# Conditioned adapter with residual layer norm: the order of the first loads and of the start-up work

## The chip, the cores and the metric

The kernel runs on one core of one Trainium2 chip. The metric is the device time of one execution in microseconds; the median of three executions is compared. A core has five engines with a queue of instructions each: PE (matrix products, into PSUM), DVE (vector work), ACT (activations and copies), POOL (elementwise work on SBUF) and SP (which here only issues transfers). ACT can issue transfers too. In the profile SP's transfers stand as queue q1 and ACT's as q10.

## What is computed

There are 128 sequences (B) of 128 positions (S) with 512 features (H), in float32. Each sequence has an id that picks one of L = 10 sets of adapter parameters. Cut to what matters:

```python
w1 = W1[language_ids]                  # (B, 512, 128)
w2 = W2[language_ids]                  # (B, 128, 512)
h = relu(einsum('bsh,bha->bsa', x, w1) + b1[language_ids][:, None, :])
adapted = einsum('bsa,bah->bsh', h, w2) + b2[language_ids][:, None, :]
r = x + adapted
mean = r.mean(-1); var = ((r - mean) ** 2).mean(-1)
normed = (r - mean) * rsqrt(var + 1e-5)
out = x + normed * gamma[language_ids][:, None, :] + beta[language_ids][:, None, :]
```

## The kernel before

**Loads.** All parameters stay in SBUF for the whole run: W1 as one tile `w1` (2.62 MB, loaded in four quarters of 640 KB by the 128-row blocks of H, in runs of 512 B, L95 to L99), W2 as one tile `w2` (two transfers of 1.3 MB, L101 to L107), the tables beta, gamma and b2 in one tile `rows` (30 rows of 2 KB, L86 to L88), b1 (`b1r`, L90) and the ids (L85). x is loaded in tiles of four sequences; the first tile, `x_0`, comes in two halves (L82, L83), the others by `load_x` (L67), with four buffers. The order on the two issuing queues is:

- SP: ids, gamma, first half of x_0, W1 quarters 0 and 1, second half of x_0, W2, x_1, x_2, x_3
- ACT: beta, b2, b1, W1 quarters 2 and 3

A helper `keep` chains the instructions of one engine, so each engine runs them in the order of the source from L85 on.

**Start-up.** DVE clamps the ids (L120 to L123) and splits the 30 table rows into three bf16 parts (L134 to L138, `parts`), and makes a selection matrix `pick` (L131, L132). Then each of the 30 rows is spread over all 128 partitions (`spread`, L152): PE multiplies a column of `pick` by `parts` into a PSUM buffer (pool `p_y`, five buffers, shared with the products of the main loop), and DVE or ACT copies it to `beta_b`, `gamma_b` or `b2_b`. `spin` (L306) issues products of no use on PE.

**Main work of one sequence b.** `transpose_x` puts x[b] into PSUM by four products with the identity (pool `p_x`, one buffer); `copy_xT` (ACT) copies it to SBUF; `stage_w1` (ACT) copies the picked set out of `w1`; `down` runs four products into `p_h` (one buffer; each float32 product shows as two instructions in the profile); `relu` (ACT) makes `hT`; `up` runs the product with `w2`, and for some sequences a product that adds b2; `residual` (DVE, L238) adds x and sums; `square` and `deviation` (ACT) and some small DVE steps give the norm; `scale` and `finish` (DVE, L282 and L291) make the output; POOL adds b2 to x (L202) and beta to x (L209) beforehand; `store` writes two sequences at a time.

**The order of the start.** It is written out by hand from L316 to L344: 12 spins, the transposes of sequence 0, b1's transpose, 22 rows spread (the transposes of sequence 1 after the sixth, then a half spin after each row), two sets of W1 staged, four spins, then down(0) to down(2) with the transposes of sequences 2 and 3 and the last eight rows, up(0), up(1), down(3). The loop from L346 on then runs each stage of the following sequences in turn, with down one sequence and up two behind the transposes.

Of the kernel before, what the change touches and what calls it, by code (L numbers as in the profile page):

```python
# [16 lines left out]
P = 128  # L17
# [6 lines left out]
def cond_resid_kernel(ctx: ExitStack, tc: tile.TileContext, x, itok, W1, b1, W2, b2, gamma, beta, out):  # L24
# [8 lines left out]
    nc = tc.nc  # L33
    B, S, H = x.shape
    L, _, A = W1.shape
    KC = H // P
# [6 lines left out]
    def keep(ins):  # L43

        engine = ins.ins.engine
        if engine in last:
            tc.add_manual_dep(ins.ins, last[engine], behind, reason="kept order")
        last[engine] = ins.ins.name
        return ins
# [20 lines left out]
    def xb(b):  # L70
        return xs[b // G][:, b % G, :]


    ids = const.tile([1, B], I32, name="ids")
    rows = rp.tile([P, H], FP, tag="r", name="rows")
    b1r = const.tile([L, A], FP, name="b1r")
    w1 = const.tile([P, L, KC, A], FP, name="w1")
# [4 lines left out]
    def load_part(lo, hi):  # L82
        keep(nc.sync.dma_start(out=x_0[:, lo:hi, :], in_=x[lo:hi].rearrange("b s h -> s b h")))  # L83

    keep(nc.sync.dma_start(out=ids, in_=itok.rearrange("(o b) -> o b", o=1)))  # L85
    keep(nc.scalar.dma_start(out=rows[0:L, :], in_=beta))  # L86
    keep(nc.sync.dma_start(out=rows[L : 2 * L, :], in_=gamma))
    keep(nc.scalar.dma_start(out=rows[2 * L : 3 * L, :], in_=b2))  # L88
    load_part(0, 2)
    keep(nc.scalar.dma_start(out=b1r, in_=b1))  # L90

    warm = const.tile([P, 1], FP, name="warm")
    nc.vector.memset(warm, 1.0)
    keep(nc.scalar.activation(warm, warm, AF.Sqrt))
    for k in range(KC):  # L95
        queue = nc.sync if k < 2 else nc.scalar
        keep(
            queue.dma_start(out=w1[:, :, k, :], in_=W1[:, k * P : (k + 1) * P, :].rearrange("l p a -> p l a"))
        )  # L99
    load_part(2, G)  # L100
    for l in range(0, L, 5):  # L101
        keep(
            nc.sync.dma_start(
                out=w2[:, l * H : (l + 5) * H].rearrange("p (l h) -> p l h", l=5),
                in_=W2[l : l + 5].rearrange("l a h -> a l h"),
# [20 lines left out]
    R = 3 * L  # L126
# [25 lines left out]
    def spread(r, copier):  # L152
        t = (beta_b, gamma_b, b2_b)[r // L]
        row = p_y.tile([P, H], FP, tag="y", name=f"row_{r}")
        pick_r = pick[:, r : r + 1].to_broadcast([96, P])
        keep(nc.tensor.matmul(row, lhsT=pick_r, rhs=parts[:96, :], start=True, stop=True))
        dst = t[:, r % L * H : (r % L + 1) * H]
        if copier is nc.scalar:
            keep(nc.scalar.copy(dst, row))
        else:  # L160
            keep(nc.vector.tensor_copy(dst, row))  # L161
# [4 lines left out]
    def lid(b, engine):  # L166
        g = b // G
        if (g, engine) not in lids:
            loads, vals = nc.values_load_multi_w_load_instructions(
                lang[0:1, g * G : (g + 1) * G],  # L170
                engines=[engine],
                min_val=0,
                max_val=L - 1,
                skip_runtime_bounds_check_because="clamped on the chip to 0..L-1 above",
            )
            for ins in loads:
                keep(ins)
            lids[g, engine] = vals
        return lids[g, engine][b % G]
# [4 lines left out]
    def stage_w1(b):  # L184
        w1s[b] = wp.tile([P, KC, A], FP, tag="w1s", name=f"w1s_{b}")
        src = w1.rearrange("p l k a -> p (l k a)")[:, bass.ds(lid(b, ET.Activation) * (KC * A), KC * A)]
        keep(nc.scalar.copy(w1s[b].rearrange("p k a -> p (k a)"), src))  # L187

    def transpose_x(b):
        pxs[b] = p_x.tile([P, KC, P], FP, tag="xT", name=f"pxT_{b}")  # L190
        for k in range(KC):
            keep(nc.tensor.transpose(pxs[b][:, k, :], xb(b)[:, k * P : (k + 1) * P], ident))  # L192

    def copy_xT(b):
        xT[b] = tp.tile([P, KC, P], FP, tag="xT", name=f"xT_{b}")
        keep(nc.scalar.copy(xT[b], pxs.pop(b)))  # L196
# [14 lines left out]
    def down(b):  # L211
        phs[b] = p_h.tile([P, P], FP, tag="h", name=f"ph_{b}")
        for k in range(KC):
            keep(
                nc.tensor.matmul(  # L215
                    phs[b], lhsT=w1s[b][:, k, :], rhs=xT[b][:, k, :], start=(k == 0), stop=(k == KC - 1)
                )
            )
        del xT[b], w1s[b]

    def relu(b):
        hT[b] = tp.tile([P, P], FP, tag="hT", name=f"hT_{b}", bufs=6)
        keep(nc.scalar.activation(hT[b], phs.pop(b), AF.Relu, bias=b1T[:, bass.ds(lid(b, ET.Activation), 1)]))  # L223

    def up(b):
        v = lid(b, ET.PE)
        ys[b] = p_y.tile([P, H], FP, tag="y", name=f"py_{b}")
        m = b2_by_matmul(b)
        if m:
            pick_b = pick[:, bass.ds(v + 2 * L, 1)].to_broadcast([96, P])  # L230
            keep(nc.tensor.matmul(ys[b], lhsT=pick_b, rhs=parts[:96, :], start=True, stop=False))  # L231
        keep(nc.tensor.matmul(ys[b], lhsT=hT[b], rhs=w2[:, bass.ds(v * H, H)], start=not m, stop=True))  # L232
        del hT[b]
# [72 lines left out]
    def spin(n, width):  # L306
        idle = p_s.tile([P, H], FP, tag="s", name="idle")
        for _ in range(n):
            keep(
                nc.tensor.matmul(  # L310
                    idle[:, :width], lhsT=ones, rhs=ones[:, 0:1].to_broadcast([P, width]), start=True, stop=True
                )
            )


    spin(12, H)  # L316
    transpose_x(0)
    transpose_b1()
    copy_xT(0)
    for r in range(22):  # L320
        spread(r, nc.scalar if r % 3 == 2 else nc.vector)
        if r == 5:
            transpose_x(1)
            copy_xT(1)
        elif r > 5:
            spin(1, H // 2)
    stage_w1(0)
    stage_w1(1)
    spin(4, H)
    for b in range(3):  # L330
        down(b)
        if b < 2:
            transpose_x(b + 2)
        relu(b)
        if b < 2:
            copy_xT(b + 2)
        for r in range(22 + 3 * b, min(25 + 3 * b, R)):
            spread(r, nc.vector)
        stage_w1(b + 2)
    up(0)  # L340
    up(1)
    down(3)
    relu(3)
    stage_w1(5)  # L344

    for i in range(3, B + U + 7):  # L346
        if i < B and i % G == 0 and i // G + 3 < NG:
            load_x(i // G + 3)
        b = i - U - 1
# [21 lines left out]
        p = g - 1  # L371
# [77 lines left out]
```

## Time and profile before

| What | Value |
| --- | --- |
| Three executions | 322.06, 322.19, 323.7 us, median 322.19 |
| The profiled execution's own time | 324.36 us |
| Its span, first to last instruction | 322.5 us |
| Mean granted PE clock | 0.984 of full |
| Busy share PE, DVE, ACT, POOL | 95%, 94%, 87%, 85% |
| Moved by DMA | 72.89 MB, mean 226 GB/s |

The profiled execution is one of its own, a little longer than the median. Some lines of the page, with the busy time of a group, the mean of one in ns, and the idle time of its engine just before with what ended it:

```profile
DVE  6928899999999999999999999999999999999994
ACT  3436999999999999999999999999999999999950
POOL 1306999999999999999999999999999999999900
...
L209 POOL TENSOR_TENSOR o<-x,beta_b 128x512 f32<-128x512 f32 x128 | 162.2, 1280 | 10.0 <-DVE beta_b L161 10.0
L202 POOL TENSOR_TENSOR r<-x,b_b 128x512 f32<-128x512 f32 x93 | 118.9, 1279 | 21.7 <-DVE b_b L161 13.4
L187 ACT COPY w1s<-w 128x512 f32 x128 | 79.3, 620 | 3.3 <-DMA w<-in_L_cond_W_dram 3.2
```

The first three lines are the busy tenths of an engine in 40 slices of some 8 us: DVE, ACT and POOL are filled from the fifth slice on, and the gaps lie in the first four. The groups say that POOL waits twice for spread rows and that ACT waits once for W1, in the start as well.

### The profile page before, as it was taken

How to read it: one execution, taken by the hardware profiler on the slowest of the kernel's cores; microseconds unless marked ns; L12 is line 12 of the kernel's file. 1: busy time of each engine (PE TensorE's matmuls, PEld its weight loads, DVE VectorE, ACT ScalarE, POOL GpSimd, SP SyncE). 2: the span in 40 equal slices, each digit the busy share in tenths (PEclk: the TensorE clock that was granted, in tenths of full speed). 3: DMA queues.
4: the chain of work that ended last, by engine and by line, in shares of the span. 5: the costliest groups of instructions: out<-in, count | busy, mean ns of one | idle time of the engine just before them, and what ended most of it. 6: DMA issues, size and time to landing. Idle time of an engine off the chain costs nothing. (4 is left out here: it accounts for less than half of the span.)

```text
span 322.5 us, 7159 instructions
## 1 busy us (share of the span) xinstructions
PE 305.1 (95%) x1889; PEld 227.0 (70%) x1890; DVE 303.8 (94%) x996; ACT 280.6 (87%) x713; POOL 274.7 (85%) x229
## 2 busy tenths in 40 slices
PE   8869999999999999999999999999999999999950
PEld 3456777777777777777777777777777777777720
DVE  6928899999999999999999999999999999999994
ACT  3436999999999999999999999999999999999950
POOL 1306999999999999999999999999999999999900
PEclk9979999999999999999999999999999999999995
DMA  7997467776666666777576666777766666633333
GB/s 207 323 384 268 186 210 259 262 259 226 210 217 223 242 229 227 261 262 251 192 231 221 235 242 224 238 262 261 244 216 212 229 227 239 221 117 131 130 125 139
DMA packets 40955, 72.89 MB, mean 226 GB/s; under 512 B 1705, under 2 KB 6836, under 8 KB 40914
## 3 DMA queue, kind: packets, MB, share of 16 engines
q1 hardware_dynamic: 38262, 71.07, 64.2%
q10 hardware_dynamic: 2652, 1.36, 1.7%
q8 instruction: 16, 0.26, 0.4%
q14 instruction: 25, 0.20, 0.2%
HBM read 38.86 MB, written 33.55 MB: 225 GB/s over the span
## 5 line engine op out<-in xcount | busy, mean ns | idle before, releaser
L209 POOL TENSOR_TENSOR o<-x,beta_b 128x512 f32<-128x512 f32 x128 | 162.2, 1280 | 10.0 <-DVE beta_b L161 10.0
L215 PE MATMUL ph<-xT,w1s 128*128 128x128 f32 x1024 | 136.3, 276 | 3.0 <-ACT w1s L187 3.0
L202 POOL TENSOR_TENSOR r<-x,b_b 128x512 f32<-128x512 f32 x93 | 118.9, 1279 | 21.7 <-DVE b_b L161 13.4
L232 PE MATMUL py<-w,hT 128*128 x256 | 131.1, 593 | 0.8 <-ACT sq L250 0.8
L215 PEld LDWEIGHTS ph<-xT,w1s 128*128 128x128 f32 x1024 | 125.5, 193 | 4.7 <-ACT w1s L187 3.5
L192 PEld LDWEIGHTS pxT<-ident,x 128*128 128x128 f32 x512 | 64.1, 141 | 66.7 <-issue 43.7
L282 DVE SCALAR_TENSOR_TENSOR py<-py,nmean,gamma_b 128x512 f32<-128x512 f32 x128 | 96.2, 752 | 0.3 <-issue 0.3
L291 DVE SCALAR_TENSOR_TENSOR o<-py,rstd,o 128x512 f32<-128x512 f32 x128 | 94.7, 741 | 1.1
L250 ACT ACTIVATE sq<-py,nmean 128x512 f32<-128x512 f32 x128 | 88.1, 688 | 2.9 <-DVE nmean L243 2.9
L196 ACT COPY xT<-pxT 128x512 f32<-128x512 f32 x128 | 73.8, 577 | 14.6 <-PE pxT L192 12.2
L187 ACT COPY w1s<-w 128x512 f32 x128 | 79.3, 620 | 3.3 <-DMA w<-in_L_cond_W_dram 3.2
L192 PE MATMUL pxT<-ident,x 128*128 128x128 f32 x512 | 77.3, 274 | 0.8 <-ACT xT L196 0.7
L238 DVE SCALAR_TENSOR_TENSOR py<-py,r 128x512 f32<-128x512 f32 x93 | 64.9, 698 | 1.6 <-PE pxT L192 0.2
L223 ACT ACTIVATE hT<-ph,b1T 128x128 f32<-128x128 f32 x128 | 47.4, 371 | 6.1 <-PE ph L215 6.1
L232 PEld LDWEIGHTS py<-w,hT 128*128 128x128 f32 x256 | 41.6, 192 | 3.4 <-ACT sq L250 1.6
L238 DVE SCALAR_TENSOR_TENSOR py<-py,x 128x512 f32<-128x512 f32 x35 | 24.3, 694 | 2.4 <-PE py L232 1.8
L250 ACT ACTIVATION_READ_ACCUMULATOR sq<-py,nmean 128x1 f32 x128 | 26.4, 206 | 0.0
L256 ACT ACTIVATE sd<-ssq,eps 128x2 f32<-128x2 f32 x64 | 18.9, 296 | 2.1
L243 DVE TENSOR_SCALAR nmean<-sum 128x1 f32<-128x1 f32 x128 | 18.9, 148 | 0.1
L231 PE MATMUL py<-parts,pick 96*128 96x512 bf16 x35 | 13.3, 381 | 0.0
L271 DVE TENSOR_TENSOR stat<-stat,y 128x2 f32<-128x2 f32 x64 | 13.2, 207 | 0.0
L238 DVE DVE_READ_ACCUMULATOR py<-py,r 128x1 f32 x93 | 13.1, 141 | 0.0
(41 smaller groups left out, 99.7 us busy)
## 6 DMA issues: line engine op xcount, KB each, us to landing
out_dram<-o SPq DMA_DIRECT2D x63, 512.0 KB, 3.4
x<-in_x_dram SPq DMA_DIRECT2D x31, 1024.0 KB, 6.1
w<-in_L_cond_W_dram SPq DMA_DIRECT2D x2, 1280.0 KB, 15.9
w<-in_L_cond_W_dram SPq DMA_DIRECT2D x2, 640.0 KB, 7.0
w<-in_L_cond_W_dram ACTq DMA_DIRECT2D x2, 640.0 KB, 9.3
x<-in_x_dram SPq DMA_DIRECT2D x2, 512.0 KB, 4.3
out_dram<-o SPq DMA_DIRECT2D x2, 256.0 KB, 2.1
rows<-in_L_cond_beta_dram ACTq DMA_DIRECT2D x1, 20.0 KB
```

Of the source, the lines that this page charges most:

```text
L187: keep(nc.scalar.copy(w1s[b].rearrange("p k a -> p (k a)"), src))
L192: keep(nc.tensor.transpose(pxs[b][:, k, :], xb(b)[:, k * P : (k + 1) * P], ident))
L196: keep(nc.scalar.copy(xT[b], pxs.pop(b)))
L202: keep(nc.gpsimd.tensor_tensor(rs[b], xb(b), b2_b[:, bass.ds(v * H, H)], ALU.add))
L209: keep(nc.gpsimd.tensor_tensor(os[g][:, j, :], xb(b), beta_b[:, bass.ds(v * H, H)], ALU.add))
L215: nc.tensor.matmul(phs[b], lhsT=w1s[b][:, k, :], rhs=xT[b][:, k, :], start=(k == 0), stop=(k == KC - 1))
L223: keep(nc.scalar.activation(hT[b], phs.pop(b), AF.Relu, bias=b1T[:, bass.ds(lid(b, ET.Activation), 1)]))
L232: keep(nc.tensor.matmul(ys[b], lhsT=hT[b], rhs=w2[:, bass.ds(v * H, H)], start=not m, stop=True))
L238: keep(nc.vector.scalar_tensor_tensor(ys[b], ys[b], 1.0, r, ALU.mult, ALU.add, accum_out=s))
L250: keep(nc.scalar.activation(sq, ys[b], AF.Square, bias=nmeans[b], accum_out=ssqs[g][:, j : j + 1]))
L282: nc.vector.scalar_tensor_tensor(ys[b], ys[b], nmeans.pop(b), gamma_b[:, bass.ds(v * H, H)], ALU.add, ALU.mult)
L291: nc.vector.scalar_tensor_tensor(o, ys.pop(b), rstds[g][:, j : j + 1], o, ALU.mult, ALU.add)
```

## The change

All of W1 goes on SP's queue, with three quarters first, then the first half of x_0, then the last quarter; ids and all three tables go on ACT's queue in front of b1. On the engines, ten rows are spread (each with its half spin) ahead of the transposes of sequence 0, six more ahead of those of sequence 1; 14 spins stand in front instead of 12, and two instead of four ahead of the first down product. Fourteen rows, instead of eight, stand between the down products, three of them copied by ACT. Four down products, instead of three, precede the first up product. The main loop is the same.

```diff
+    def load_w1(k):
+        keep(
+            nc.sync.dma_start(out=w1[:, :, k, :], in_=W1[:, k * P : (k + 1) * P, :].rearrange("l p a -> p l a"))
+        )
-    keep(nc.sync.dma_start(out=ids, in_=itok.rearrange("(o b) -> o b", o=1)))
-    keep(nc.scalar.dma_start(out=rows[0:L, :], in_=beta))
-    keep(nc.sync.dma_start(out=rows[L : 2 * L, :], in_=gamma))
-    keep(nc.scalar.dma_start(out=rows[2 * L : 3 * L, :], in_=b2))
-    load_part(0, 2)
+    keep(nc.scalar.dma_start(out=ids, in_=itok.rearrange("(o b) -> o b", o=1)))
+    for k, table in enumerate((beta, gamma, b2)):
+        keep(nc.scalar.dma_start(out=rows[k * L : (k + 1) * L, :], in_=table))
     keep(nc.scalar.dma_start(out=b1r, in_=b1))
...
     for k in range(KC):
-        queue = nc.sync if k < 2 else nc.scalar
-        keep(
-            queue.dma_start(out=w1[:, :, k, :], in_=W1[:, k * P : (k + 1) * P, :].rearrange("l p a -> p l a"))
-        )
+        if k == KC - 1:
+            load_part(0, 2)
+        load_w1(k)
     load_part(2, G)
...
-    spin(12, H)
+    def spread_some(lo, hi):
+        for r in range(lo, hi):
+            spread(r, nc.scalar if r % 3 == 2 else nc.vector)
+            spin(1, H // 2)
+
+    spin(14, H)
+    spread_some(0, 10)
     transpose_x(0)
     transpose_b1()
     copy_xT(0)
-    for r in range(22):
-        spread(r, nc.scalar if r % 3 == 2 else nc.vector)
-        if r == 5:
-            transpose_x(1)
-            copy_xT(1)
-        elif r > 5:
-            spin(1, H // 2)
+    spread_some(10, 16)
+    transpose_x(1)
+    copy_xT(1)
     stage_w1(0)
     stage_w1(1)
-    spin(4, H)
-    for b in range(3):
+    spin(2, H)
+    for b in range(4):
         down(b)
...
-        for r in range(22 + 3 * b, min(25 + 3 * b, R)):
-            spread(r, nc.vector)
+        for r in range(16 + 5 * b, min(21 + 5 * b, R)):
+            spread(r, nc.scalar if r % 5 == 3 else nc.vector)
         stage_w1(b + 2)
     up(0)
     up(1)
-    down(3)
-    relu(3)
-    stage_w1(5)
```

## The prediction

> **What bounds the kernel now.** I read the busy time by stages first, then the timeline of the first 34 us, then the DMA queues in narrow stretches.
>
> ```profile
> 15.00:19.00 4.00, 0.99 (x4) 0.37 (x4) 1.11 (x2) 0.84 (x2) 0.00 (x0) 0.94 1.07 375
> 19.00:23.00 4.00, 4.00 (x21) 3.52 (x22) 0.82 (x2) 1.77 (x4) 0.00 (x0) 0.63 1.05 386
> ...
> 31.00:35.00 4.00, 3.89 (x28) 3.32 (x29) 2.24 (x9) 3.75 (x11) 4.00 (x5) 1.00 0.02 3
> 35.00:45.00 10.00, 10.00 (x63) 7.32 (x62) 9.85 (x34) 9.56 (x25) 10.00 (x9) 1.00 0.81 295
> ...
> 200.00:300.00 100.00, 100.00 (x641) 76.34 (x639) 99.15 (x336) 94.86 (x246) 96.68 (x79) 1.00 0.62 212
> ```
>
> Columns: stage, its length, busy us of PE, weight loads, DVE, ACT, POOL, then granted clock, DMA share, GB/s. From 35 us on DVE is 99% busy and nothing in the change touches it there, so the end moves with the moment at which DVE becomes packed. That moment is the residual of sequence 3 (L238) at 33.78 us: it is the last of DVE's longer stalls. At 15 to 19 us every compute engine is nearly idle, and the clock halves afterwards. The timeline of DVE, ACT and PE says why:
>
> ```profile
> 3.10 0.42 DVE L134 CAST parts<-rows 30x512 bf16<-30x512 f32 x1 [0.23 <-DMA rows<-in_L_cond_b_dram]
> ...
> 7.05 4.28 DVE L161 COPY beta_b<-row 128x512 f32<-128x512 f32 x7 [0.15 <-PE row L156]
> ...
> 18.16 1.14 ACT L187 COPY w1s<-w 128x512 f32 x2 [3.19 <-DMA w<-in_L_cond_W_dram]
> ...
> 18.83 2.08 PE L215 MATMUL ph<-xT,w1s 128*128 128x128 f32 x8 [2.95 <-ACT w1s L187]
> ...
> 33.78 0.70 DVE L238 SCALAR_TENSOR_TENSOR py<-py,x 128x512 f32<-128x512 f32 x1 [1.25 <-PE py L232]
> ```
>
> Start, duration, instruction, and in brackets the idle time and its releaser. Two loads matter: the tables (landed by 3.10), which feed the spread products, and W1 (landed by 18.16), which feeds the first down product at 18.83. W1 is the wait that ends last. The third view is the DMA queues in three stretches, 2.8 to 4.1, 4.1 to 5.7 and 5.7 to 7 us (q1 is SP's, q10 ACT's; packets, MB, share):
>
> ```profile
> q1 hardware_dynamic: 165, 0.34, 75.6%
> q10 hardware_dynamic: 1, 0.00, 0.1%
> ...
> q1 hardware_dynamic: 790, 0.52, 101.3%
> q10 hardware_dynamic: 20, 0.01, 2.2%
> ...
> q1 hardware_dynamic: 451, 0.23, 64.6%
> q10 hardware_dynamic: 346, 0.18, 50.5%
> ```
>
> ACT issued b1 at 1.72 us and its first W1 quarter at 2.17, yet ACT's queue moves nothing until 4.1 (b1's few packets) and no W1 until 5.7. SP's half of x_0 (issued 1.50) and its first W1 quarter (1.95) went first. So a transfer on one queue waited while larger ones issued before it on the other were worked off: about 1.6 us per W1 quarter (4.2 to 5.8 in the packet records).
>
> **The change, part by part.** I follow three moments: S, the first cast of the tables (L134, 3.10); t0, the first down product (18.83); and residual 3 (33.78).
>
> W1 moves to the head of SP's queue. SP's queue nearly alone moved 335 packets between 5.2 and 5.7 us, or 670 per us; both queues together moved 1141 from 10 to 12 us, or 570. W1 is 5120 packets of 512 B: 7.6 to 9.0 us. The x_0 half ahead of the last quarter is 0.52 MB at 386 GB/s (18 to 29 us), 1.4. First packets come about 1.3 us after issue (x_0: 1.50 to 2.84) and 0.9 goes to the ramp. W1 lands at 0.74+1.3+0.9+1.4+(7.6 to 9.0)+0.5 = 12.4 to 13.8, against 18.16. The x_0 half lands near 11. W2 follows the same bytes as before, so it lands no later than the present 23.0.
>
> Tables and ids move behind W1's quarters. ACT now issues ids, beta, gamma, b2, b1, at about 0.3 us each after a first of 0.62; b2 goes out near 2.04. SP's first two quarters go out from 0.74 and 1.25. The third should be held back: SP's x_0 rest was blocked from 3.34 to 6.45 when some 2800 packets were outstanding, and three quarters are 3840. So two quarters are ahead of b2. S = 2.1 (first packet) + 2x1.6 + 0.3 (beta and gamma) + 0.57 (b2's first packet at 2.53 to the cast) = 6.2. Lower bound, with nothing ahead: 2.04+1.7 = 3.8. Upper bound, with three quarters and the x_0 half ahead: 2.1+4.8+1.35+0.3+0.57 = 9.1. I take 6.2 because b1's and W1's packets above are the nearest rows. Queued behind the cast on DVE are all splits, pick and every spread copy; PE waits for pick, and behind that wait stand the x_0 transposes and all down products. Ids, ahead of it, add nothing, since L120 to L123 take 0.8 us and land before b2. The extra issue on ACT only delays the table load (2.10), long before its first copy.
>
> [...]
>
> From S to t0, by the new order: splits and pick 3.2 (3.10 to 6.29), first product and its latency 0.45, seven DVE copies 4.28, b1T 0.17, row 10's copy 0.61 (it frees one of five PSUM buffers for row 15), row 15 with its spin 0.43, four transposes 0.60, ACT's xT copy 0.59, w1s copy 0.62, handovers 0.25: 11.2. That puts t0 at 17.4. W1 (13.8 at worst) is then hidden by the spread work with at least 2 us to spare, since w1s is read at 16.7; x_0 (11) is needed at 12.8.
>
> The clock. The 14 spins end near 6.2 (the 12 ended at 5.77; two more at 0.22) and pick is ready at S+3.2 = 9.4, so PE idles 3.2 us. The present 2.95 us of idling was followed by half clock for about 3.4 us (0.50 from 19 to 21). A row with its spin takes 0.33 us at full clock (8.67 to 9.00), 0.66 at half; the copies leave 0.41 per row. In 3.4 us that is 5.2 rows instead of 8.3: 3.1x0.41 = 1.3 us. Bounds 0 and 1.3; I take 1.1, as some of the window may fall before the first row. t0 = 18.5.
>
> [...]
>
> From t0 to residual 3: four down products at 0.89 (31.61 to 32.50), two sets of transposes at 0.44 (33.58 to 34.02) and 14 rows at 0.22 are 7.5 on PE; three up at 1.08 (25.72 to 26.79) 3.24; from the transposes of sequence 4 to residual 3 3.94 (29.84 to 33.78). Sum 14.7, against 14.95 now: six more rows stand here (1.3) where 1.7 went to half clock. Moving down(3) ahead changes its place, not its price. DVE's 11 copies take 6.9 from t0+1.8 and end at t0+8.7, beside PE's first up (done t0+8.8); were they later, residual 0 would slip, but ACT's square has about 1 us of room before it delays the xT copy of sequence 4. W2 is first read at t0+7.7 = 26. POOL starts on b2_b at t0+8.7 = 27.2, now 27.37: no loss.
>
> Sum: 18.5+14.7 = 33.2 for residual 3, so the end moves by -0.6 us. The profiled execution (324.36 us, span 322.5) becomes 323.8 with a span of 321.9; the median shown, 322.19, is 2.2 below that execution, and moves to 321.6.
>
> **The rivals.**
> Forecast: the table wait takes W1's place, with the clock drop. 321.6, own range 320.6 to 322.8 (S within 0.7, the clock price 0.6 to 1.3). Chance 0.44.
> Same tables, but PE keeps its clock: t0 = 17.4, residual 3 at 32.1, -1.7, so 320.5. The idle stretch is as long as one that halved it. 0.15.
> Tables pass at once: S = 3.8. Then x_0 decides: landed 11, transposes, row 15's chain and copies 4.6 to t0 = 15.6; residual 3 at 30.3, -3.5, so 318.7. For it: beta's and b2's packets left 1.1 us after issue; against it: nothing large was ahead of them. 0.16.
> Slower than before: the tables queue behind the third quarter too, or behind the x_0 half. Its place is the wait of L134; it decides once S passes 6.8 with half clock. S = 7.8 gives t0 = 20.1, +1.0, 323.2; S = 9.1 gives t0 = 21.4, +2.3, 324.5. For it: the two queues alternated transfer by transfer in the stretches above, and four table transfers alternating with SP's would let b2 out after the x_0 half. Against it: the held-back third quarter. 0.20.
> Left over, mostly a slower start that I don't see: 0.05.
>
> **How the numbers follow.** Range 318.9 to 324.3: it takes in the no-clock-drop case and most of both outer ones. A half per cent, 1.6 us, is about what a measurement of this kernel can tell from no change; faster means below 320.6, slower above 323.8. Faster: the tables-pass case, half of the full-clock case and a little of the forecast, 0.30. Slower: half of the last rival and the left-over, plus the forecast's tail where my chain of handovers is too short, 0.23. Same: 0.47.
>
> **What would show it.** L134 starts near 6.2 with its releaser the DMA of the tables (at 3.8 the first rival is right, at 8 or more the slower one); ACT's queue shows no 2 KB packets until SP's first 2500 have been worked on. W1 releases nothing: L189 of the changed kernel starts on PE or ACT's own order. PE idles about 3 us before its first row, then rows with spins come at 0.66 us. The first down product is near 18.5, residual 3 near 33.2, and DVE is packed after it. Wrong would be a wait in the loop after 35 us that is not there now, or x_0 releasing PE's first transposes.

## The result, and the profile after

The changed kernel is 1.3% slower: median 327.39 us (326.88 to 327.81, 4 runs) against 322.94 us (322.06 to 324.5, 4 runs), ratio 1.0132, 95% interval 1.0084 to 1.018. Its profiled execution took 326.88 us with a span of 325.0 (324.36 and 322.5 before), so the two profiled executions lie 2.5 us apart and the medians 4.5. The first difference is worked out below; for the second, experiment 8 has the likely reason.

The stages of the changed kernel, with the same columns as before (stage, length, busy us of PE, weight loads, DVE, ACT, POOL, clock, DMA share, GB/s):

```profile
6.00:10.00 4.00, 0.67 (x4) 0.10 (x1) 2.06 (x4) 0.00 (x0) 0.00 (x0) 0.91 1.19 287
10.00:15.00 5.00, 3.92 (x13) 1.90 (x14) 3.58 (x8) 0.66 (x2) 0.00 (x0) 0.50 1.10 342
15.00:19.00 4.00, 4.00 (x23) 2.25 (x22) 3.24 (x6) 2.27 (x4) 1.27 (x2) 0.86 1.05 387
...
200.00:300.00 100.00, 100.00 (x640) 76.34 (x639) 99.13 (x334) 95.01 (x247) 96.59 (x79) 1.00 0.63 215
```

The hole has moved: it was at 15 to 19 us, and is now at 6 to 10, with half clock (0.50) from 10 to 15. From 200 to 300 us DVE is as busy as before (99.13 against 99.15 us). The steps of the start in the timelines of DVE, PE and ACT:

```profile
7.83 0.41 DVE L136 CAST parts<-rows 30x512 bf16<-30x512 f32 x1 [5.05 <-DMA rows<-in_L_cond_b_dram]
...
11.08 0.61 PE L158 MATMUL row<-parts,pick 96*128 96x512 bf16 x1 [4.42 <-DVE pick L134]
...
20.89 1.14 ACT L189 COPY w1s<-w 128x512 f32 x2 [0.17 <-issue]
...
21.56 1.16 PE L217 MATMUL ph<-xT,w1s 128*128 128x128 f32 x8 [1.25 <-ACT w1s L189]
...
36.31 0.70 DVE L240 SCALAR_TENSOR_TENSOR py<-py,x 128x512 f32<-128x512 f32 x1 [1.25 <-PE py L234]
```

W1 releases nothing any more: the copy out of it at 20.89 had 0.17 us of idling before it, and its last packet started at 13.3. The tables release instead: DVE sat idle for 5.05 us until b2 had landed, PE for 4.42 behind it. Residual 3, the moment from which DVE is packed, went from 33.78 to 36.31, and these 2.53 us are the whole difference of the two profiled executions. The DMA queues in three stretches, 4.3 to 5.5, 5.5 to 6.5 and 6.5 to 7.2 us:

```profile
q1 hardware_dynamic: 698, 0.35, 116.6%
q10 hardware_dynamic: 13, 0.01, 2.9%
...
q1 hardware_dynamic: 494, 0.25, 112.9%
q10 hardware_dynamic: 18, 0.02, 6.2%
...
q1 hardware_dynamic: 351, 0.18, 108.3%
q10 hardware_dynamic: 21, 0.02, 10.2%
```

ACT's queue (q10) has 13 to 21 packets in each stretch, rows of the tables and packets of 4 bytes, called completion writes here (10 with each table and 16 with each quarter of W1, the last of them behind the data), while SP's queue moves W1. In the packet records, on the timeline's zero, W1 starts at 1.85, beta at 4.18, gamma at 5.43, b2 at 6.49, b1 at 7.05, though all four of ACT's had been issued by 2.82. So the tables came one by one: 2.33 us after W1's first packet, then 1.25 and 1.06 later. How much of W1 had started when beta and when b2 did, is shown by the packets from 1.84 to 4.18 and from 1.84 to 6.49 (q10's 41 are beta, gamma, their completion writes and b2's first):

```profile
q1 hardware_dynamic: 996, 0.51, 77.5%
...
q1 hardware_dynamic: 2236, 1.14, 95.1%
q10 hardware_dynamic: 41, 0.04, 3.0%
```

A quarter of W1 has 1280 packets. Without the first quarter's 16 completion writes, 2220 packets of W1 had started when b2 did, less than two quarters, and the second quarter's completion writes came only at 6.75 to 7.44. So a table did not wait until whole quarters had been moved. The author's estimate, from the three steps of 2.33, 1.25 and 1.06 us: the two queues took turns here, and one transfer of ACT's was let in for each one of SP's. By that, the third quarter, whose issue ended at 4.20, was let in ahead of b2, whose issue had ended at 2.44. This order is inferred, from the steps and from experiment 5; the packets don't show it.

### The profile page after: what moved, and what is told of

Read it like the earlier page. It is cut to its first block, busy times and chain, and to the rows that moved or that the text cites. A ratio compares the mean times of both kernels' runs of the same rounds, so it can differ in the third digit from the quotient of the medians.

```text
span 325.0 us, 7160 instructions
## 1 busy us (share of the span) xinstructions
PE 305.6 (94%) x1889; PEld 226.5 (70%) x1890; DVE 303.9 (94%) x995; ACT 280.6 (86%) x714; POOL 274.4 (84%) x229
## 5 line engine op out<-in xcount | busy, mean ns | idle before, releaser
L198 ACT COPY xT<-pxT 128x512 f32<-128x512 f32 x128 | 73.7, 576 | 13.3 <-PE pxT L194 10.6
L158 PE MATMUL row<-parts,pick 96*128 96x512 bf16 x30 | 11.3, 446 | 4.4 <-DVE pick L134 4.4
L233 PE MATMUL py<-parts,pick 96*128 96x512 bf16 x35 | 13.3, 381 | 0.0
```

## The experiments

Each kernel is followed by the moments at which DVE's first cast, the first down product and residual 3 start. In all kernels but the sixth, the profiled time is residual 3 plus 290.4 to 290.8 us, so residual 3 tells the time. A profiled execution's time is 1.73 to 2.13 us longer than its span, in the sixth 2.86.

| Kernel | Cast | First down | Residual 3 | Profiled, us | Median (range; runs) | Ratio to before (95%) |
| --- | --- | --- | --- | --- | --- | --- |
| before | 3.10 | 18.83 | 33.78 | 324.36 | 322.94 (322.06 to 324.5; 4) | |
| changed | 7.83 | 21.56 | 36.31 | 326.88 | 327.39 (326.88 to 327.81; 4) | 1.0132 (1.0084 to 1.018) |
| 1 tables first | 3.09 | 19.82 | 34.57 | 325.33 | 324.2 (322.17 to 325.33; 10) | 1.0002 (0.9973 to 1.0031) |
| 2 old loads, new order | 3.05 | 18.80 | 35.96 | 326.53 | 326.59 (326.4 to 327.0; 4) | 1.0065 (1.0046 to 1.0084) |
| 3 new loads, old order | 7.80 | 24.51 | 37.96 | 328.33 | 327.87 (327.25 to 328.33; 4) | 1.0095 (1.0075 to 1.0115) |
| 4 long spin | 7.95 | 19.53 | 34.28 | 324.75 | 324.68 (324.36 to 324.8; 10) | 1.0001 (0.9982 to 1.0019) |
| 5 half quarters | 7.20 | 21.77 | 36.52 | 327.05 | 327.05 (1 run) | |
| 6 x_0 earlier | 3.15 | 15.82 | 30.75 | 322.76 | 322.32 (321.63 to 323.12; 12) | 0.9942 (0.9913 to 0.9972) |
| 7 tables first, spin | 3.09 | 17.27 | 32.02 | 322.66 | 322.59 (322.39 to 323.41; 10) | 0.9965 (0.9931 to 0.9999) |
| 8 before, spin | 3.10 | 18.86 | 32.31 | 322.76 | 322.84 (322.42 to 323.44; 10) | 0.9961 (0.993 to 0.9992) |
| 9 beta early | 3.09 | 15.09 | 30.62 | 321.15 | 321.81 (321.15 to 322.7; 12) | 0.9939 (0.9911 to 0.9967) |
| 10 best loads, old order | 3.13 | 20.76 | 34.21 | 324.62 | 324.33 (324.08 to 324.83; 10) | 1.001 (0.9981 to 1.0039) |

The kernel before, timed beside experiments 1 to 4, had a median of 324.42 us (322.47 to 326.04); beside 5 to 8, 323.96 (322.14 to 326.64); beside 9 and 10, 324.33 (321.98 to 326.13). The ratios are against such runs, so the changed kernel's ratio, from four runs of before, is not to be set against them digit by digit: against these medians its 327.39 would be some 0.9 to 1.1% more, and not 1.3.

**Experiment 1, tables first.** Beta and b2 ahead of W1 on SP's queue, gamma behind the ids on ACT's.

```diff
     for k, table in enumerate((beta, gamma, b2)):
-        keep(nc.scalar.dma_start(out=rows[k * L : (k + 1) * L, :], in_=table))
+        queue = nc.scalar if k == 1 else nc.sync
+        keep(queue.dma_start(out=rows[k * L : (k + 1) * L, :], in_=table))
```

> Theory A (the tables wait their turn behind W1's quarters, and PE's clock falls while it waits for pick): with beta and b2 ahead of W1 on SP's queue and gamma on ACT's, L134-like first cast starts near 3.2 us instead of 7.8, PE has no long idle time and no half clock; the first half of x_0 lands near 12.6 and decides; first down product near 17.1, residual 3 near 31.8 against 36.3, so 4.5 us less than the changed kernel: 322.4. Theory B (the new order of work on PE and ACT is what costs): the cast starts early, but the first down product and residual 3 move by less than 1.5 us: 325.4 or more.

The cast came at 3.09, as expected of theory A, which shows where the table wait is from. The rest missed: the first down product stood at 19.82 and not at 17.1, and the median only equals the kernel before. A row of PE's timeline says why,

```profile
12.19 1.09 PE L195 MATMUL pxT<-ident,x 128*128 128x128 f32 x4 [2.39 <-DMA x<-in_x_dram]
```

and its stages from 10 to 19 us show the price:

```profile
10.00:15.00 5.00, 2.81 (x10) 1.63 (x11) 1.90 (x4) 0.89 (x2) 2.48 (x2) 0.68 1.10 340
15.00:19.00 4.00, 3.93 (x14) 2.06 (x12) 2.02 (x3) 1.46 (x3) 0.00 (x0) 0.55 1.06 389
```

The first half of x_0, behind three quarters of W1, is the next wait: PE idled 2.39 us (9.80 to 12.19), and the clock was half from 11.8 to 18.6, by the means of 0.68 and 0.55 above (the transposes take 1.09 instead of 0.60 us).

**Experiments 2 and 3, one half of the change alone.** The load lines (up to the last load of x_0) of one kernel are put into the other; nothing else is edited.

> The changed kernel's order of work with the old loads. Theory A: cast at 3.1, W1 lands at 18.2 as before, first down product 18.8; sixteen rows are done by about 14, so PE idles some 4 to 5 us and the following products run at half clock for 3.4 to 6.8 us: residual 3 at 34 to 36, 324.6 to 326.6. Theory B: the order of work alone gives the changed kernel's time, 327. If neither the order nor the clock matters: as before, 322.2 to 324.4.

> The old order of work with the changed kernel's loads. Theory A: cast at 7.8; the x_0 transposes, which stand first on PE, wait for x_0 at about 11.8, and all rows stand behind them; 22 rows then take about 9 us, first down product 21 to 23, residual 3 at 35 to 37: 326 to 327.6. Theory B: the old order gives the old time, 322.2 to 324.4.

The first down product and residual 3 of the second kernel, then PE's transposes and residual 3 of the third:

```profile
18.80 2.08 PE L215 MATMUL ph<-xT,w1s 128*128 128x128 f32 x8 [4.85 <-ACT w1s L187]
35.96 0.70 DVE L238 SCALAR_TENSOR_TENSOR py<-py,x 128x512 f32<-128x512 f32 x1 [1.25 <-PE py L232]
```

```profile
11.96 1.09 PE L194 MATMUL pxT<-ident,x 128*128 128x128 f32 x4 [5.81 <-DMA x<-in_x_dram]
37.96 0.70 DVE L240 SCALAR_TENSOR_TENSOR py<-py,x 128x512 f32<-128x512 f32 x1 [1.25 <-PE py L234]
```

Each half alone loses too, by the intervals 0.5 to 0.8% and 0.8 to 1.2%. The new order with the old loads does its rows early and then idles 4.85 us for W1; from there to residual 3 it takes 17.2 us instead of the 14.75 of experiment 4 below, and the clock is half until 23.8 (0.74 from 15 to 19 us, 0.50 from 19 to 23, 0.90 from 23 to 27). The new loads with the old order wait for x_0 with everything behind it, and half clock lasts 10.24 us there (0.50 from 15 to 19 us, 0.96 from 19 to 23); first down product (24.51) and residual 3 (37.96) came 1 to 1.5 us later than the latest that was expected. Theory B's numbers are near these results in experiment 2 (326.59 against 327), so this one alone doesn't tell the theories apart; experiment 3 does, as the old order gave 327.87 and not the old time.

**Experiment 4, long spin.** The loads stay as in the changed kernel; PE is only kept busy until `pick` is there.

```diff
-    spin(14, H)
+    spin(34, H)
```

> 34 spins instead of 14, so that PE is busy until pick is ready near 11. Theory A: the loads stay as they are (cast at 7.8), but rows with spins come at 0.33 us and not 0.64 us, first down product near 19.0 instead of 21.6, residual 3 near 33.8: 324.4, that is 2.5 us less than the changed kernel. If the clock is no part of the loss: 326.9 to 327.4 as the changed kernel.

The stage from 10 to 15 us, and the first down product in the timeline:

```profile
10.00:15.00 5.00, 5.00 (x30) 2.77 (x29) 4.15 (x10) 1.64 (x3) 0.00 (x0) 1.00 1.10 342
```

```profile
19.53 1.16 PE L217 MATMUL ph<-xT,w1s 128*128 128x128 f32 x8 [1.03 <-ACT w1s L189]
```

The clock is full from 10 to 15 us (0.50 in the changed kernel, third column from the end). With the cast 0.12 us later, the first down product comes 2.03 us earlier, so the clock is worth 2.15 us in the changed kernel; its median fell by 2.7 us. As expected of theory A, within 0.5 us.

**Experiment 5, half quarters.** Each W1 quarter is issued as two transfers of five sets each.

```diff
-        keep(
-            nc.sync.dma_start(out=w1[:, :, k, :], in_=W1[:, k * P : (k + 1) * P, :].rearrange("l p a -> p l a"))
-        )
+        for l in range(0, L, 5):
+            keep(
+                nc.sync.dma_start(
+                    out=w1[:, l : l + 5, k, :],
+                    in_=W1[l : l + 5, k * P : (k + 1) * P, :].rearrange("l p a -> p l a"),
+                )
+            )
```

> The changed kernel with each W1 quarter issued as two transfers of 320 KB on the same queue. Theory A (the two queues take turns transfer by transfer, so each table waits for one of SP's transfers): the tables now wait behind three halves and not three quarters, so the first cast starts at 5.3 to 5.8 us instead of 7.8. Theory C (the tables wait for a share of bytes, or until SP's queue has been filled): the cast stays at 7.8. The time is not the question here; it can lie between 323.5 and 326.9, as the clock falls or not.

The cast came at 7.20, which neither theory expected. The packet records show beta from 3.31 (4.18 in the changed kernel), gamma from 4.03 (5.43) and b2 from 4.80 (6.49): the steps became 0.7 to 0.8 us from 1.1 to 1.25. But b2 needs all its ten packets; eight started by 5.16 and two only at 5.99 and 6.24. With SP's transfers halved to 320 KB the steps were shorter, as theory A has it. Why two packets were a step behind is open.

**Experiment 6, x_0 earlier.** Experiment 1 with the first half of x_0 behind two quarters of W1, and spins where PE would idle.

```diff
-        if k == KC - 1:
+        if k == KC - 2:
             load_part(0, 2)
...
     spread_some(0, 10)
+    spin(2, H)
     transpose_x(0)
...
-    spin(2, H)
+    spin(6, H)
     for b in range(4):
```

> Tables ahead of W1 as in the first experiment, the first half of x_0 behind two quarters of W1 instead of three, and spins where PE would idle (2 ahead of the x_0 transposes, 6 instead of 2 ahead of the first down product). Theory A: cast 3.1, x_0 transposes at about 10.4 with no long idle time, no half clock; W1 lands about 14.7 and the first down product stands near 15.4, residual 3 near 30.1 against 33.8 before: 320.7, some 2 to 4 us less than the kernel before. Theory B (the new order of work costs): no faster than the kernel before.

This beats both kernels, by 0.3 to 0.9% against the kernel before. The first down product (15.82) and residual 3 (30.75) came near the expectation, yet the profiled execution took 322.76 and not 321.3 (30.75 plus 290.6). About 1.0 of these 1.4 us lies outside the span, which is 319.9 us long; why is open. For the rest, POOL's timeline and the waits of DVE between residual 3 and the end show a candidate:

```profile
26.47 1.27 POOL L205 TENSOR_TENSOR r<-x,b_b 128x512 f32<-128x512 f32 x1 [12.05 <-DMA x<-in_x_dram]
```

```profile
DVE py L241 <- POOL r L205: 0.9, 2, 0.8
DVE py L241 <- POOL o L212: 0.4, 1, 0.4
```

The columns of the waits are us in total, times, longest. POOL, idle before, begins its b2 additions when x_1 lands (26.47), no earlier than in experiment 7 (26.64), and DVE then waits 1.3 us for it. From residual 3 to the end of the span it takes 289.15 us, 0.4 to 0.6 more than in the others.

**Experiment 7, tables first with a spin.** Experiment 1 with 12 spins ahead of the x_0 transposes.

```diff
     spread_some(0, 10)
+    spin(12, H)
     transpose_x(0)
```

> The first experiment with 12 spins ahead of the x_0 transposes, which cover its 2.4 us of idle PE. Theory A with the clock: the transposes stay at 12.3, but all at full clock; first down product 17.1 instead of 19.8, residual 3 near 31.8 instead of 34.6: 322.4, that is 2.5 us less than the first experiment's profiled execution. If the clock is not what held it: 324.2 to 325.3 as there.

First down product 17.27, residual 3 32.02, 322.66 us, with the clock at 1.00 from 15 to 19 us (0.55 in experiment 1): the clock was what held experiment 1, 2.67 us in the profiled executions.

**Experiment 8, the kernel before with a spin.**

```diff
     stage_w1(1)
-    spin(4, H)
+    spin(18, H)
     for b in range(3):
```

> The kernel before with 18 spins instead of 4 ahead of the first down product, which cover the 2.95 us that PE idles for W1. First down product at 18.8 as before but at full clock, residual 3 near 32.1 instead of 33.8: 322.6 for the profiled execution, and the times lie within 1 us of each other, where those of the kernel before spread over 3.5 us. If the clock does not matter: 322 to 326, as the kernel before.

```profile
18.86 1.16 PE L215 MATMUL ph<-xT,w1s 128*128 128x128 f32 x8 [0.18 <-ACT w1s L187]
32.31 0.70 DVE L238 SCALAR_TENSOR_TENSOR py<-py,x 128x512 f32<-128x512 f32 x1 [1.25 <-PE py L232]
```

As expected: W1 still decides the first product (18.86), but from there to residual 3 it takes 13.45 us instead of 14.95, with the clock at 1.00 from 15 to 27 us. The ten times lie within 1.0 us, while the kernel before spread over 4.5 us beside them. Of the 71 runs of the kernel before that were timed beside the experiments, the 22 with a mean granted clock of 0.985 or more took 321.98 to 323.34 us, the 32 with 0.981 or less 323.7 to 326.64, and the 17 between them 322.08 to 325.68. So a part of its runs, the profiled one among them, seem to pay 1.5 us or more for the clock, and others not; only the profiled one's start is on record.

The spins alone gain as much over the kernel before (ratio 0.9961) as experiment 7 does (0.9965). Beyond them, the change as mended in experiment 6 is worth 0.5 us (medians 322.32 and 322.84, timed together).

**Experiment 9, beta early.** Experiment 6 with POOL's beta additions for sequences 0 to 3 put first.

```diff
     up(1)
+    for b in range(4):
+        add_beta(b)
...
-        if on(b):
+        if on(b) and b > 3:
             add_beta(b)
```

> The sixth kernel, with POOL's beta additions of sequences 0 to 3 put ahead of its first b2 addition, which waits for x_1 until 26.5 us. If POOL's late start is what gives back part of the earlier start there (DVE waited 1.3 us for POOL after residual 3): those waits go, residual 3 stays near 30.8, and the time falls by about 1.3 us against the sixth kernel: 321.0. If POOL was only named and DVE waits for something else: 322.3 as there.

The two waits above are gone, with 0.4 us of waiting for POOL left elsewhere; residual 3 is at 30.62, and the profiled time, 321.15, is again residual 3 plus 290.5. The spans of the two profiled executions lie 0.7 us apart (319.2 and 319.9), and the medians 0.5, in different runs, not 1.3; the two ratios can't be told apart. So POOL's late start cost some 0.6 us at most. A new wait stands in the start:

```profile
23.59 1.10 PE L235 MATMUL py<-w,hT 128*128 x2 [0.55 <-DMA w<-in_L_cond_W_dram]
```

That is the first up product, waiting for W2.

**Experiment 10, the best loads with the old order.** The load lines of experiment 6 in the kernel before, with 32 spins instead of 12 in front.

> The loads of the sixth kernel with the old order of work, and 32 spins instead of 12 in front, so that PE stays busy until x_0 is there. If the new order of work (rows ahead of the transposes) is worth something once W1 goes first: the x_0 transposes stand first and wait until about 10.4, all 22 rows behind them take 9 us, first down product about 19.9, residual 3 about 33.2, 2.4 us later than in the sixth kernel: 323.8. If only the loads matter: the sixth kernel's 322.3.

First down product 20.76, residual 3 34.21, median 324.33, 2.0 us more than experiment 6. The x_0 transposes stood first and ran at 10.80; 22 rows and their copies behind them took the rest, and the first product came 0.9 us later than expected. So with these loads the new order of work is worth something. With the old loads and no spins it lost, though its tables landed early (experiment 2).

## Why the prediction was wrong

The mechanism had the right places, the tables' wait and then the clock. Its sizes were too small, so that the shift came out as +2.53 us in the profiled executions and not -0.6, and the time lies outside the range. By the prediction's own steps:

- *W1 is hidden.* Right. It landed near 14 us and released nothing. The 0.9 us for the ramp in its sum was the author's estimate; the trace before moved 76 GB/s from 2 to 3 us and 291 from 3 to 4, against 386 from 18 to 29 us.
- *S = 6.2, with two quarters ahead of b2.* Measured 7.83, 1.63 more. The step that failed first is this wait: "The third should be held back", hence 2x1.6 + 0.3 = 3.5 us from W1's first packet to b2's. It measured 4.64 (1.85 to 6.49), in three steps and not two, though the third quarter's issue was held to 4.20. The reading behind it, that a transfer waits until the larger ones ahead "were worked off", was wrong in the trace before already: ACT's W1 started at 5.69, when 690 of the 1280 packets of SP's first quarter had. Nor did ACT's queue wait "until SP's first 2500 have been worked on"; beta started after 996. The last rival's turns fit, and it put S at 7.8 for a third quarter and got 323.2 from it; that b2 stood behind that quarter is inferred. The other term that was too small is the 0.57 from b2's first packet to the cast, which measured 1.34. (The prediction's packet times 2.84 and 2.53 stand 0.24 above the timeline, which makes this term 0.81 in the trace before, and its 2.1 for W1's first packet 1.85; the two cancel in the sum.)
- *From S to t0, 11.2.* Measured without the clock 11.58 (experiment 4: 7.95 to 19.53), 0.4 more.
- *The clock, 1.1.* Measured 2.15 (13.73 us from cast to first product in the changed kernel, less 11.58). The bound of 1.3 was wrong: it took half clock to last 3.4 us as in the trace of before, and here it lasted 6.83 (9.27 to 16.09), with 4.42 us of idling (6.67 to 11.08) and not 3.2.
- *From t0 to residual 3, 14.7.* Measured 14.75.
- *The base.* 1.63 + 0.38 + 1.05 + 0.05 gives the 3.11 us between 33.2 and 36.31. The time missed by 5.8. The other 2.7 come from taking a shift worked out from one profiled execution off a median 2.2 us below it. That execution had paid for half clock, which hid part of the change's cost, and most of the runs shown probably had not; experiment 8 makes this likely. The changed kernel pays in all its runs (mean clocks 0.976 to 0.978), and its median is 0.5 above its profiled one.
- *The rivals.* "Tables pass at once" is refuted. "PE keeps its clock" is refuted by the 0.50 from 10 to 15 us, with 4.42 us of idling. Of the slower rival, place and S were right and the price was not.

## What to carry to other kernels

A small load that much work waits for belongs ahead of the large ones, or on the same queue in front of them: on a second queue the small loads here started one by one, at 4.18, 5.43 and 6.49 us, though they had been issued by 2.44, and the cast stood at 7.83; with beta and b2 in front on SP's queue (experiment 1) it stood at 3.09. When a load is moved out of the way, look at what it is put ahead of and at what the waiting engine does meanwhile: here PE's idling of 4.42 us cost another 2.15 us in half clock, and cheap spins that end when the data land took it back (experiment 4). Compare shifts between executions that had the same clock, and test the order of work and the order of loads both together and apart: here each of them alone was a loss, and the pair, with tables and x_0 early and spins over PE's idling, a gain of 0.5 us over the old kernel with spins. A cheap cure tried alone first, as in experiment 8, tells what the large change is worth beyond it.

## What the runs showed of the hardware that was not expected

- Tables of 20 KB on ACT's queue, issued by 2.44 us, started one by one at 4.18, 5.43 and 6.49 while SP's queue moved quarters of 640 KB. With 320 KB halves the steps were 0.7 to 0.8 us instead of 1.1 to 1.25. By the packets started (996, 1702, 2220 of W1), the tables did not wait for whole quarters to be moved.
- In the start, half clock lasted 3.41 us in the clock records of the kernel before (18.55 to 21.96), 6.83 in those of the changed one (9.27 to 16.09) and 10.24 in experiment 3, that is one, two and three times 3.41. It went with idle stretches of PE of 2.39, 2.95, 3.34, 4.42, 4.85 and 5.81 us, and not with those of 0.68 to 1.25. In the 3.41 us just before each such drop PE was busy for 0.36 to 1.46 us (0.68 in the kernel before, 0.81 in the changed one); in the start, the clock stayed full after the other such windows, counted in steps of 3.41 us from the edges of these records, with 2.16 us or more. The lengths of the idle stretches and these busy times separate the drops from the rest equally well; no run here tells which of the two decides.
- In the kernel before, SP's queue nearly alone moved W1's 512-byte packets at 349 GB/s (5.2 to 5.7 us), and the two queues together at 291 (10 to 12 us, 572 and 569 packets).
